# A graph kernel whose own planner orders its instructions: other durations in the planner's table

## Chip, cores and metric

The kernel runs on one core of one Trainium2 chip. The metric is device time in microseconds for one execution; the time given for the kernel before is the median of three runs. Besides those, one execution was profiled.

The core has five engines that each run their own instruction stream in order and wait for each other by semaphores: TensorE (PE in the profile, its weight loads PEld), VectorE (DVE), ScalarE (ACT), GpSimd (POOL) and SyncE (SP). Here GpSimd does little but issue indirect DMAs, and SyncE little but issue ordinary ones.

## What is computed

There are 16 graphs of 1024 nodes with 64 features each, and an adjacency matrix of 1024 x 1024 float32 per graph, about eight neighbours to a node. Four layers follow each other, each on a layer-normed and rectified copy of the features, each added to the features:

```python
h = jnp.maximum(_layernorm(x, axis=-1), 0.0)
x = x + _L0_gnn_ref(h, adj, W)             # (adj @ h) @ W.T
h = jnp.maximum(_layernorm(x, axis=-1), 0.0)
x = x + _L1_gnn_ref(h, adj, ...)           # m = mlp(h); msg = relu(adj @ m); a gated unit of (msg, h)
h = jnp.maximum(_layernorm(x, axis=-1), 0.0)
x = x + _L2_gnn_ref(h, adj, weight, K, b)  # Chebyshev: h, adj @ h, 2 adj @ (adj @ h) - h
h = jnp.maximum(_layernorm(x, axis=-1), 0.0)
x = x + _L3_gnn_ref(h, adj, nodemask, ...)
```

The last layer thins each node's list of neighbours (in lists of more than ten every k-th is removed, in both directions), takes for each feature the quartiles over the values of the neighbours left, with weights 1/4, 1/2 and 1/4, adds them to the node's own value and runs a small two-layer network.

## The kernel before

**Stages of a graph.** Each stage is a Python generator (a "chain") that yields one instruction at a time.

- *Transposing* (`transposing`): eight blocks of the adjacency matrix are loaded by SyncE into two buffers (`block`), transposed by TensorE and copied by ScalarE into tiles `AT`, of which there are 15; a graph takes eight.
- *Coding* and *listing* (`coding`, `lists`): the sign of the transposed tiles is packed into words, and VectorE finds from them the up to 24 neighbours of each node (`top`, `cand`, `more`, then three MAX8 and two MATCH_REPLACE8 for each of eight row tiles, then some forty small instructions, the last of which writes `many`). This is called the list block below. A graph's list is made some graphs ahead of its use. After the last one, `longest` finds the nodes with long lists.
- *Layers* (`layers`): two chains, one for the even and one for the odd graphs, run layers 0 to 2. A chain holds one tile `X` and ends with the last sum `pay<-X,bank` on VectorE, a norm on ScalarE, and the stores of `table` and `rows` by SyncE. The next graph of the chain begins with the load of `X`. Three passes over a graph's eight `AT` tiles (`bank<-AT,nodes`) are in it; the third gives the tiles back.
- *Gathering* (`gathering`, `gathers`): GpSimd gathers for each graph ten neighbours of eight row tiles from `table`, 80 indirect DMAs, into one of two buffers `G`, slot after slot.
- *Quantiling* (`quantiles`): VectorE begins with `hits<-G,pay`, runs a sorting network of min and max over slots of 128 x 512 values, ping-pong between `G` and the one buffer `net`, and ends with the coefficients `coef<-off`. Then the sorted slots are weighed by the coefficients (six instructions on VectorE, 24 on ScalarE).
- *Dense* (`dense`): TensorE sums the weighed slots (`bank<-G,c`), after which `G` is given back, and runs the small network; the result is stored by SyncE (`out<-yo`), and one of three `pay` buffers is given back.
- *Long lists*: at the end the nodes with more than eleven neighbours, gathered from all graphs (`whom`), pass through gathering, quantiling and dense again in four batches with longer networks; that is 122 more gathers, and nine scatters of results.

**What sets the order.** The class `Weave` is a planner that runs while the kernel is built. It keeps a clock for every engine. Each chain offers its next instruction; the earliest start of an instruction is the later of the time at which its engine is free (`free`) and the time at which its operands are ready (`ready`). The engine on which something can start earliest is served; among the instructions that could start on it within `SLACK` (0.1 us) of that, the one whose chain has the lowest key wins. Keys are graph numbers with an offset: layers and transposing `b - 3`, coding the same, listing `b - 2`, dense `b`, gathering and quantiling `b + 1`; so a layer of graph 7 goes before a quantile instruction of graph 4.

An instruction has two numbers: `cost`, for which it occupies its engine, and `later`, the time after that until its result can be used. Use on another engine adds 0.15 us. `Line.cost` gives both for each kind of instruction; a gather has its own, `GATHER`: it occupies GpSimd for so long, and lands 2.2 us later. Each instruction is made in the planned order and tied to the one before it on its engine:

```python
for other in self.last.get(line, ()):
    self.behind(ins, other)
```

So the order on every engine is the planner's, while the times at which instructions really run come from the hardware. In the kernel before, VectorE and ScalarE instructions have a `cost` and no `later`.

In the profile nearly every instruction bears line 303, the line at which a chain's instruction is made; tiles tell them apart. Gathers have line 634, stores line 640 and scatters line 1324.

Of the kernel before, what the change touches and what calls it, by code (L numbers as in the profile page):

```python
# [98 lines left out]
EXTRA = 6 * NT  # L99
BIG = 1e30  # L100
SLACK = 0.1
GATHER = 1.33
RANK = 3.0
SHARE = 3
LONGEST = 512
# [74 lines left out]
def network(n, places, beam=200):  # L180
# [4 lines left out]
    for layer in needed(batcher(n), range(places)):  # L185
        new = {}
        for buf, (cost, ops) in states.items():
            classes = {}
            for a, b, la, lb in layer:
# [73 lines left out]
class Op:  # L263
# [5 lines left out]
    def __init__(self, line, make, writes, reads, cost, later=0.0, after=()):  # L269
        self.line, self.make, self.cost, self.later, self.after = line, make, cost, later, after  # L270
        self.writes, self.reads = [place(a) for a in writes], [place(a) for a in reads]
# [16 lines left out]
class Line:  # L288
# [17 lines left out]
    def cost(self, method, out, reads, kwargs):  # L306
        if method == "dma_start":
            return 0.4, 2.0 + out.nbytes() / 150e3
        n = max(a.free_size() for a in [out] + reads)
        extra = "accum_out" in kwargs  # L310
        if self.name == "DVE":
            fixed = {"match_replace": 0.145, "max": 0.155}.get(method, 0.155)
            return fixed + n / 960 + 0.08 * extra, 0.0
        if self.name == "ACT":
            scalars = sum(hasattr(kwargs.get(k), "ap") for k in ("bias", "scale"))
            return 0.225 + n / 1400 + 0.09 * scalars + 0.19 * extra, 0.0
        if self.name == "PE":
            if method == "transpose":
                return 0.19, 0.25
            n = out.free_size()  # L320
            if mybir.dt.size(reads[0].dtype) == 2:
                return 0.06 + n / (4400 if out.shape[0] == C else 2200), 0.3
            pair = n == 512 and reads[0].shape[0] == P and out.shape[0] == C
            return (0.58 if pair else max(0.34, 0.06 + n / 545)), 0.3
        return 1.33, 2.2


# [140 lines left out]
class Fast:  # L468
# [162 lines left out]
    def gather(self, out, table, at, reads):  # L631

        def make():
            return self.nc.gpsimd.indirect_dma_start(  # L634
                out=out, out_offset=None, in_=table, in_offset=bass.IndirectOffsetOnAxis(ap=at, axis=0))
        return Op(self.G, make, [out], [reads, at], GATHER, 2.2)

# [1345 lines left out]
```

## Time and profile before

| | us |
|---|---|
| median of three runs (lowest, highest) | 2125.57 (2113.96, 2135.73) |
| the profiled execution | 2138.34 |
| its span, from first to last instruction | 2136.4 |
| first gather starts | 130.9 |
| last gather starts | 2092.2 |

| engine | busy us |
|---|---|
| PE | 1533.9 |
| PEld | 717.0 |
| DVE | 1632.9 |
| ACT | 1073.5 |
| POOL | 1437.7 |

The mean granted clock of TensorE was 0.782 of full speed. Durations are of one profiled execution. A line of a timeline gives the start, the duration, the engine, the source line, the operation, what it writes and reads, and in brackets the idle time of the engine before it with the event that ended it. A merged line (x4) has the duration from the first start to the last end. An instruction's own duration overlaps that of its neighbour on VectorE and ScalarE, so a sum of durations is more than the time the engine needs for them.

### The profile page before, as it was taken

The numbers are of one execution on the slowest core, as the hardware profiler recorded it, in microseconds if no ns is written. First come the engines' busy times: TensorE is split into PE (matmuls) and PEld (weight loads), VectorE is DVE, ScalarE is ACT, GpSimd is POOL, SyncE is SP. The second block draws the span as 40 slices with busy tenths as digits, with TensorE's granted clock in tenths as the row PEclk, the third lists the DMA queues.
The fourth block names the chain that finished last, engine by engine and source line by source line (L and its number), as shares of the span: only waits on it lengthen the run. The fifth ranks groups of instructions, "written<-read, shape, count | busy, mean of one in ns | idle before, by whom it ended". The sixth has DMA issues, their size and how long they took to land. (4 is left out here: it accounts for less than half of the span.)

```text
span 2136.4 us, 22993 instructions
## 1 busy us (share of the span) xinstructions
PE 1533.9 (72%) x6172; PEld 717.0 (34%) x6172; DVE 1632.9 (76%) x4293; ACT 1073.5 (50%) x2921; POOL 1437.7 (67%) x1441
## 2 busy tenths in 40 slices
PE   6978677869787879787887878787978872233303
PEld 2443323333434343343333333334343331111302
DVE  2661687978888887888886969787788899949646
ACT  3654647566666655566656474757466532011000
POOL 2047776777676767577777667676757777776772
PEclk9979796978788796989796979787779786555555
DMA  4242625252625252444334353525252314121110
GB/s 121 70 86 57 117 38 94 59 105 52 104 51 104 52 93 58 58 94 61 88 62 94 50 94 61 104 48 99 51 92 50 43 31 41 30 31 24 32 27 11
DMA packets 246840, 140.93 MB, mean 66 GB/s; under 512 B 76048, under 2 KB 223952, under 8 KB 246704
## 3 DMA queue, kind: packets, MB, share of 16 engines
q1 hardware_dynamic: 195664, 88.11, 18.4%
q0 software_dynamic: 46096, 48.62, 17.5%
q10 hardware_dynamic: 4944, 2.66, 0.5%
q8 instruction: 53, 0.87, 0.2%
q14 instruction: 83, 0.68, 0.1%
HBM read 120.10 MB, written 19.17 MB: 65 GB/s over the span
## 5 line engine op out<-in xcount | busy, mean ns | idle before, releaser
L634 POOL DMA_INDIRECT G<-table,pay x1402 | 1408.0, 1004 | 652.6 <-issue 351.6
L303 PE MATMUL bank<-AT,nodes 128*64 128x512 f32 x2048 | 605.7, 671 | 88.1 <-ACT nodes L303 78.6
L303 PEld LDWEIGHTS bank<-AT,nodes 128*64 128x64 f32 x2048 | 181.6, 153 | 386.2 <-issue 223.6
L303 PE MATMUL bank<-G,c 128*128 128x512 f32 (+3 forms) x382 | 172.1, 590 | 183.4 <-DVE G L303 179.4
L303 PE MATMUL bank<-c,block 128*128 128x128 f32 x976 | 223.5, 349 | 106.8 <-DMA block<-in_adj 60.5
L303 ACT ACTIVATE AT<-bank 128x512 f32<-128x512 f32 x256 | 149.5, 588 | 188.9 <-PE bank L303 186.4
L303 PEld LDWEIGHTS bank<-c,block 128*128 128x128 f32 x976 | 147.3, 176 | 229.2 <-issue 137.7
L303 DVE TENSOR_TENSOR G<-G 128x512 f32<-128x512 f32 (+3 forms) x313 | 200.1, 674 | 2.8
L303 ACT ACTIVATE nodes<-X,off,ri 128x64 f32<-128x64 f32 x360 | 141.0, 429 | 42.6 <-DVE off L303 41.3
L303 DVE TENSOR_TENSOR net<-G 128x512 f32<-128x512 f32 (+6 forms) x240 | 150.6, 672 | 11.3 <-ACT G L303 9.3
L303 PEld LDWEIGHTS bank<-G,c 128*128 128x128 f32 x382 | 72.1, 226 | 254.5 <-DVE G L303 129.1
L303 ACT ACTIVATE G<-G,coef 128x64 f32<-128x64 f32 x384 | 98.2, 336 | 110.0 <-DVE coef L303 109.8
L303 ACT ACTIVATE sq<-X,st 128x64 f32<-128x64 f32 x360 | 124.6, 346 | 49.7 <-DVE st L303 34.1
L303 ACT ACTIVATE there<-AT 128x1024 f16<-128x1024 f32 x128 | 132.1, 1050 | 0.9
L303 ACT ACTIVATE wide<-bank 64x512 f32<-64x512 f32 x128 | 75.1, 586 | 108.7 <-PE bank L303 107.5
L303 DVE TENSOR_TENSOR G<-net 128x512 f32<-128x512 f32 (+7 forms) x189 | 117.2, 667 | 0.7
L303 DVE TENSOR_TENSOR G<-G,net 128x512 f32<-128x512 f32 (+3 forms) x177 | 111.4, 679 | 0.9
L303 PE MATMUL bank<-wide,wg 64*64 64x512 f32 (+1 forms) x192 | 110.1, 656 | 0.8 <-ACT wide L303 0.4
L303 DVE SCALAR_TENSOR_TENSOR G<-bad,G 128x512 f32<-128x512 f32 (+1 forms) x176 | 109.8, 693 | 0.0
L303 DVE MAX8 L<-cand 128x8 f16<-128x103 f16 x384 | 91.9, 263 | 8.8
L303 PE MATMUL bank<-there,c 128*64 128x512 f16 x256 | 79.8, 449 | 24.3 <-DVE there L303 24.1
L303 DVE TENSOR_REDUCE st<-X 128x8 f32<-128x512 f32 x48 | 32.9, 686 | 82.5 <-DMA X<-in_x 81.4
(200 smaller groups left out, 2235.0 us busy)
## 6 DMA issues: line engine op xcount, KB each, us to landing
block<-in_adj SPq DMA_DIRECT2D x121, 512.0 KB, 4.2
G<-table,pay POOLq DMA_INDIRECT x1402, 2.8
rows<-pay SPq DMA_DIRECT2D x16, 632.0 KB
table<-pay SPq DMA_DIRECT2D x16, 264.0 KB, 5.2
X<-in_x SPq DMA_DIRECT2D x16, 256.0 KB, 8.5
out<-yo SPq DMA_DIRECT2D x16, 256.0 KB, 2.6
G<-in_adj SPq DMA_DIRECT2D x3, 512.0 KB, 10.7
G<-in_adj ACTq DMA_DIRECT2D x3, 512.0 KB, 9.2
```

What stands on the lines that cost most here:

```text
L303: return Op(self, lambda: f(*args, **kwargs), writes, reads, cost, later)
L634: return self.nc.gpsimd.indirect_dma_start(out=out, out_offset=None, in_=table, in_offset=bass.IndirectOffsetOnAxis(ap=at, axis=0))
```

## The change

The planner's durations are set anew. No chain, key, buffer or instruction is written differently. For VectorE, ScalarE and the transposes, matmuls and gathers the time of occupation becomes shorter, and for VectorE and ScalarE a `later` of 0.09 and 0.10 us is split off.

```diff
-GATHER = 1.33
+GATHER = 1.29
...
         if self.name == "DVE":
-            fixed = {"match_replace": 0.145, "max": 0.155}.get(method, 0.155)
-            return fixed + n / 960 + 0.08 * extra, 0.0
+            fixed = {"match_replace": 0.165, "max": 0.095}.get(method, 0.07)
+            return fixed + n / 960 + 0.08 * extra, 0.09
         if self.name == "ACT":
             scalars = sum(hasattr(kwargs.get(k), "ap") for k in ("bias", "scale"))
-            return 0.225 + n / 1400 + 0.09 * scalars + 0.19 * extra, 0.0
+            return 0.13 + n / 1400 + 0.09 * scalars + 0.19 * extra, 0.1
         if self.name == "PE":
             if method == "transpose":
-                return 0.19, 0.25
+                return 0.165, 0.25
             n = out.free_size()
             if mybir.dt.size(reads[0].dtype) == 2:
                 return 0.06 + n / (4400 if out.shape[0] == C else 2200), 0.3
             pair = n == 512 and reads[0].shape[0] == P and out.shape[0] == C
-            return (0.58 if pair else max(0.34, 0.06 + n / 545)), 0.3
+            return (0.51 if pair else max(0.26, 0.06 + n / 640)), 0.3
         return 1.33, 2.2
```

For a VectorE instruction on 512 values a row, the planner's occupation goes from 0.688 to 0.603 us; the time until its result can be used stays nearly the same, 0.693.

## Prediction

> **What bounds the kernel now.** I read the page's busy shares first, then the waits, then GpSimd's, SyncE's and VectorE's timelines around two graphs.
>
> ```profile
> PE 1533.9 (72%) x6172; PEld 717.0 (34%) x6172; DVE 1632.9 (76%) x4293; ACT 1073.5 (50%) x2921; POOL 1437.7 (67%) x1441
> ...
> POOL 2047776777676767577777667676757777776772
> ...
> L634 POOL DMA_INDIRECT G<-table,pay x1402 | 1408.0, 1004 | 652.6 <-issue 351.6
> ```
>
> No engine is full, but GpSimd is never long idle after the first tenth. A gather is 1.00 us busy and, at "issue", 0.25 us more (351.6/1402), so 80 of a graph need at least 100 us. In the timeline the gathers of graphs 4, 9 and 14 (counted from 0) begin at 566.65, 1121.21 and 1683.98: 111 to 113 us a graph. The one at 1683.98, in the order of time from SyncE, GpSimd and VectorE (start, duration, engine):
>
> ```profile
> 1676.98 0.37 SPq L640 DMA_DIRECT2D table<-pay  x1
> ...
> 1683.98 0.94 POOL L634 DMA_INDIRECT G<-table,pay  x1 [3.03 <-DVE more L303]
> ...
> 1792.53 1.15 POOL L634 DMA_INDIRECT G<-table,pay  x1 [1.49 <-DVE net L303]
> ```
>
> GpSimd waits for graph 14's table, whose store was issued 7.0 us earlier (the VectorE name in brackets is only the last event). From there GpSimd runs to its last gather at 2092.2 with few waits, the longest 9.28 us, and the kernel ends 44 us later. So the layers of a graph (in pairs, through all engines) set the pace until 1684, and GpSimd sets the end from there. VectorE at graph 9, then at 14:
>
> ```profile
> 1106.26 0.68 DVE L303 TENSOR_TENSOR pay<-X,bank 128x512 f32<-128x512 f32 x1
> ...
> 1107.77 0.45 DVE L303 TENSOR_REDUCE coef<-off 128x72 f32<-128x288 f32 x1
> ...
> 1116.18 0.68 DVE L303 SCALAR_TENSOR_TENSOR cand<-top,c 128x504 f16<-128x504 int32 x1 [3.26 <-ACT cand L303]
> ...
> 1125.93 0.69 DVE L303 TENSOR_REDUCE st<-X 128x8 f32<-128x512 f32 x1 [6.10 <-DMA X<-in_x]
> ...
> 1149.59 0.17 DVE L303 TENSOR_TENSOR many<-dil,notes 128x8 f32<-128x8 f32 x1
> ...
> 1159.91 0.33 DVE L303 TENSOR_TENSOR hits<-G,pay 128x160 f32<-128x160 f32 x1 [0.21 <-DMA G<-table,pay]
> ...
> 1667.51 0.68 DVE L303 TENSOR_TENSOR pay<-X,bank 128x512 f32<-128x512 f32 x1
> ...
> 1670.83 0.45 DVE L303 TENSOR_REDUCE coef<-off 128x72 f32<-128x288 f32 x1
> ```
>
> The last sum of graph b (`pay<-X`) and the end of graph b-2's quantiles (`coef`, after which G is only weighed and read) fall together. Then comes the list block of a later graph, alone, up to `many`, with VectorE waiting inside it; then `hits`, the next quantiles. Hence G of graph b-2 comes free just when the table of graph b lands.
>
> **The change, part by part.** No instruction is added or removed on VectorE (4,039 in both programs), TensorE or GpSimd; ScalarE gets 35 instead of 33 table loads. The rest is order, so I compared the order of the two built programs engine by engine, and priced what is moved by its rows here.
>
> *Pay earlier.* Ahead of the last sum of graph 9 stand 23 network instructions fewer, 14.0 us by their own records (a 128x512 one starts 0.60 us after its neighbour; the page's mean of 0.69 overlaps it); for graphs 5 to 14 it is 13 to 17 us. It is one shift, not one per graph: with the pace unchanged it gives the table nothing that GpSimd can use, because of the next item.
>
> *Quantiles later.* Ahead of `coef` of graph 7 stand 107 instructions more, nearly all one list block: 24 MAX8 5.7 us, 16 MATCH_REPLACE8 4.0 and their value loads 1.5 (16 x 92 ns), 8 short MAX8 1.1, five wide ones 2.9, 41 small 8.1, 13 of layers and coding 3.6: 26.9 us. Other graphs have 106 to 110 more, graphs 5 and 9 only 39. `coef` of graph 12 has 142 more: 23 of layers 9.2, the list block 23.5 (same rows), and 25 of the step that finds the long rows, 12.4: 45.1 us. `hits` has next to none more before graph 12, so the same quantile work is spread over the list block.
>
> *Who waits for that.* Gathers of graph b write G of graph b-2, slot by slot. Graph 15 shows how far ahead they may run: they began at 1792.5, `coef` of graph 13 at 1800.5, 8.0 us. For graph 9: coef 7 at 1107.8 + 26.9 - 8.0 = 1126.7 against 1121.2 now; a delay of some 5 us, covered, since `hits` of that graph comes later still. For graph 14 nothing covers it: 1670.8 + 45.1 - 8.0 = 1707.9 against 1684.0, **24 us later**. If VectorE keeps waiting at its present rate in the moved block (94 us busy of 110 a graph: 33.4 + 60.1 in two windows), 45.1 becomes 52.8 and the delay 32. I take 24, the value nearest to records of the very instructions. After that all is GpSimd: graph 15 follows 14 without a hold (`coef` of 13 has only 2.0 us more ahead), and the tail's order on VectorE is the same from `coef` of 13 on. So +24 us passes to the end.
>
> *Pace.* What the layers' chain gains or loses is unpriced by any row. Above nothing: the list block's waits, X 81.4 us and `cand` 37.2 us over 16 graphs, 7.4 a graph, may be filled by network work that now stands there. Below: between the last sum and the next graph's first layer sum, VectorE's own work was 7 to 10 us and becomes 12.5 to 16.8 in most graphs (+5 to +7), while the rest of the loop shrinks from 80.5-82.7 to 74-79 (-3 to -8). The two nearly cancel, so I take zero; ends -6 to +3 us a graph over the 12 graphs from 2 to 14.
>
> *Queues.* SyncE: in five graphs a block load now stands between the rows' store and the next X load; it waits for TensorE to leave its buffer (1149.7 us in 119 waits, 9.7 each), and X behind it, and VectorE at `st<-X`: 0 to 49 us, taken at 0 since X is used late; it is part of the slower rival. GpSimd: one gather and one scatter change places in the tail, within 1 us. Two more table loads are 2 x 1.28 us on an engine half idle: 0, 2.6 without that cover. PE's order changes in thousands of places; its share is in the pace.
>
> [...] Gathers took 0.95 us each beside the list block (30.53/32, 660 to 705 us) and 0.99 beside the network (51.39/52, 705 to 772). If all 30 of the former met network work, a graph would lose 1.0 us, 12 in all; as the number of network instructions is the same, I take 0. [...]
>
> *Sum.* The profiled execution took 2138.3 us (span 2136.4), 12.8 above the median of the runs. 2138.3 + 24 = 2162 on its scale, 2125.6 + 24 = **2150** for the median; own range 2138 to 2165.
>
> **Rivals.** *Faster: the list block's waits are filled.* For it: VectorE stands 7.4 us a graph in that block, and network work is placed around it. Against: part of it is waiting for the layers' own chain, which no order shortens. GpSimd's floor is some 104 us a graph (graph 10's gathers ran 1237.2 to 1340.2 plus issue) against 110, so at most 6 x 12 = 72. With 4.5 a graph: 2125.6 + 24 - 54 = 2096; at most 2078. It decides above 2 us a graph (24/12).
>
> *No change: pace pays for the delay.* 1 to 3 us a graph saved: -12 to -36, 2126 in the middle. Against: it needs a coincidence.
>
> *Much slower: the layers' chain itself gets longer,* by 3 us a graph from the 5 to 7 us more between the two sums, with X late in five graphs: 24 + 36 = 60, 2186. Against: the shorter rest.
>
> That the order would not change is excluded: VectorE's two lists differ in most places.
>
> **Numbers.** Within 1% (2104 to 2147) is about what a measurement here can't tell from no change. Forecast 0.38, faster 0.29, no change 0.20, much slower 0.13. The forecast's range begins inside the 1% band: 0.05 of its 0.38 goes there. Faster 0.29, same 0.25, slower 0.46. The range drops a tenth on each side: the fastest third of the gain (below 2088) and the end of the much slower case (above 2186).
>
> **What would show it.** `coef` of graph 7 after a list block and some 27 us later against `many`; GpSimd's start of graph 14 held by G, not by the table store, some 24 us after 1684; tables 110 us apart; the tail from there as long as now (452 us from 1684 to the end). It would be wrong if tables came 107 us apart or less, or 113 or more; if waits for X and `cand` on VectorE vanished and the pace followed; or if gathers could run much further than 8 us ahead of `coef`.

## The result, and the profile after

The changed kernel takes 2235.3 us (median of four runs, 2215.77 to 2238.58) beside 2126.7 for the kernel before in the same session (2113.96 to 2135.73): a ratio of 1.0496, with a 95% interval of 1.0415 to 1.0577. Between the two medians lie 108.6 us, more than four times the 24 that were forecast, and the time is outside of the range.

| profiled execution, us | before | after | difference |
|---|---|---|---|
| span | 2136.4 | 2232.0 | +95.6 |
| tables of graph 4 to 14, per graph | 111.7 | 117.4 | +5.8 |
| store of graph 14's table | 1677.0 | 1732.5 | +55.5 |
| from that store to the graph's first gather | 7.0 | 53.2 | +46.2 |
| first gather of graph 14 | 1684.0 | 1785.8 | +101.8 |
| from there to the end (the tail) | 452.4 | 446.2 | -6.2 |

So up to graph 14 a hundred microseconds were lost, about half of them in the distance of the tables and half in a wait of GpSimd behind the last of them, and the tail gave 6 back. Below, this wait is called the hold: the time from the store of a graph's table to its first gather. It is not at graph 14 alone: from graph 3 to 13 it is 28 to 41 us in the changed kernel and 5 to 9 in the kernel before.

Distances, holds and tails are read from one profiled execution of each kernel. Those of the kernels on ordinary chips lie from 12 us below to 15 above the median of their kernel's runs, and the kernel before was profiled 12 us above its own. By these numbers I estimate some 1 us a graph of uncertainty in each distance, and small differences between distances are not read.

The page of the changed kernel, its busy times, GpSimd's row of the 40 slices and the gathers' group:

```profile
PE 1558.6 (70%) x6172; PEld 715.5 (32%) x6172; DVE 1628.1 (73%) x4293; ACT 1077.2 (48%) x2923; POOL 1426.4 (64%) x1441
...
POOL 2047677737676757767676757675757477776772
...
L634 POOL DMA_INDIRECT G<-table,pay x1402 | 1396.3, 996 | 757.6 <-issue 337.9
```

VectorE and GpSimd work no longer than before: 1628.1 us against 1632.9, and 1426.4 against 1437.7. ScalarE has 3.7 us more, and TensorE 24.7 (1558.6 against 1533.9) with the same number of instructions. The span is 95.6 us longer. What GpSimd has more is idle time before its gathers, 757.6 against 652.6, and the idle time put down to "issue" is less (337.9 against 351.6).

The list of waits of the changed kernel (us in total, times, longest):

```profile
POOL G L634 <- PE bank L303: 118.6, 45, 16.3
PE bank L303 <- DMA block<-in_adj: 116.6, 28, 9.2
...
POOL G L634 <- DVE net L303: 95.2, 7, 30.5
...
DVE of_h L303 <- ACT wide L303: 73.8, 13, 12.3
```

Before, GpSimd waited 13.9 us for `bank`, 10.8 for `net` and 37.9 for its tables; for tables it now waits 0.3. It waits for the instructions that read or write `G` last: dense's matmuls and the sorting network. That is the hold by the buffer that the prediction named. The second line belongs to transposing and the fourth to the layers; they stood at 60.5 us (10 times) and 23.8 before.

Graph 14 in the timelines of SyncE, GpSimd and VectorE of the changed kernel:

```profile
1722.86 0.69 DVE L303 TENSOR_TENSOR pay<-X,bank 128x512 f32<-128x512 f32 x1 [1.41 <-PE bank L303]
...
1732.53 0.37 SPq L640 DMA_DIRECT2D table<-pay  x1
...
1785.78 1.15 POOL L634 DMA_INDIRECT G<-table,pay  x1 [23.94 <-DVE net L303]
...
1792.28 0.44 DVE L303 TENSOR_REDUCE coef<-off 128x72 f32<-128x288 f32 x1
```

The last sum of graph 14 and the end of graph 12's quantiles, which stood 3.3 us apart before, are 69.4 apart. The table has long landed (by the page, 4.7 us after its issue in the median) when GpSimd's first gather starts, 53.2 us after that store and 6.5 us before `coef`.

Where the other half went is read from the windows view, each kernel from its table 4 to its table 14. After the window and its length come the busy times with the numbers of instructions, then the granted clock, the DMA share and GB/s; the kernel before first.

```profile
560.20:1677.00 1116.80, 925.95 (x3664) 422.43 (x3663) 916.54 (x2440) 678.99 (x1869) 795.52 (x797) 0.82 0.41 74
```

```profile
558.10:1732.50 1174.40, 937.53 (x3656) 422.90 (x3656) 905.83 (x2436) 681.67 (x1869) 797.21 (x801) 0.79 0.43 71
```

VectorE (the third busy time) does nearly the same work in both, 916.5 and 905.8 us for ten graphs. It is idle for 200.3 us of the first and 268.6 of the second. The 57.6 us that ten graphs take longer are idle time of VectorE, 68.3 more, less 10.7 of busy time. The same view from the start to the first gather of graph 14, before and after:

```profile
0.00:1683.98 1683.98, 1371.94 (x5522) 627.80 (x5522) 1286.33 (x3528) 996.47 (x2686) 1128.64 (x1141) 0.83 0.41 76
```

```profile
0.00:1785.78 1785.78, 1413.50 (x5600) 632.87 (x5600) 1310.79 (x3649) 1016.88 (x2736) 1123.01 (x1142) 0.80 0.42 72
```

Of the 101.8 us up to that gather VectorE is busy for 24.5 and idle for 77.3.

### The profile page after: what moved, and what is told of

Its sections match the earlier page's. It is cut to its first block, busy times and chain, and to the rows that moved or that the text cites. A ratio compares the mean times of both kernels' runs of the same rounds, so it can differ in the third digit from the quotient of the medians.

```text
span 2232.0 us, 23001 instructions
## 1 busy us (share of the span) xinstructions
PE 1558.6 (70%) x6172; PEld 715.5 (32%) x6172; DVE 1628.1 (73%) x4293; ACT 1077.2 (48%) x2923; POOL 1426.4 (64%) x1441
## 5 line engine op out<-in xcount | busy, mean ns | idle before, releaser
L634 POOL DMA_INDIRECT G<-table,pay x1402 | 1396.3, 996 | 757.6 <-issue 337.9
L303 PE MATMUL bank<-G,c 128*128 128x512 f32 (+3 forms) x382 | 183.9, 604 | 209.9 <-DVE G L303 209.9
L303 PE MATMUL bank<-c,block 128*128 128x128 f32 x976 | 225.8, 360 | 142.2 <-DMA block<-in_adj 116.6
L303 PEld LDWEIGHTS bank<-AT,nodes 128*64 128x64 f32 x2048 | 167.3, 153 | 379.6 <-issue 235.0
L303 ACT ACTIVATE G<-G,coef 128x64 f32<-128x64 f32 x384 | 95.6, 336 | 102.3 <-DVE coef L303 102.0
L303 DVE SCALAR_TENSOR_TENSOR of_h<-bank,bhn,wide 64x512 f32<-64x512 f32 x32 | 23.8, 744 | 121.3 <-ACT wide L303 73.8
L303 PE MATMUL bank<-wide,wg 64*64 64x512 f32 (+1 forms) x192 | 101.1, 616 | 2.9 <-ACT wide L303 2.0
L303 DVE TENSOR_TENSOR net<-G,net 128x512 f32<-128x512 f32 (+3 forms) x140 | 87.4, 665 | 0.1
```

What stands on the lines that cost most here:

```text
L303: return Op(self, lambda: f(*args, **kwargs), writes, reads, cost, later)
L634: return self.nc.gpsimd.indirect_dma_start(out=out, out_offset=None, in_=table, in_offset=bass.IndirectOffsetOnAxis(ap=at, axis=0))
```

## Experiments

The prediction had the quantiles late in the order and took the pace of the layers (the distance of the tables) as unchanged. The theory after the result: the late quantiles themselves cost the pace, some 6 us a graph, besides the hold of GpSimd at graph 14. Against it stood that the shorter durations spoil the order in some other way, by VectorE's and ScalarE's numbers (the title of the change) or by TensorE's; that a shift of the quantiles is harmless where the layers are undisturbed; and that the time goes inside one tie or one engine.

To choose kernels I read the order that each would have, with VectorE's work summed between two points (us of work; no time is in it). Two numbers describe it: how far `coef` of graph b-2 stands behind the last sum of graph b, and how far the last sum of graph b stands behind `yo` of graph b-3, which frees its `pay` buffer.

```
                                      coef behind last sum   pay free ahead
before                                      -1 to 3             31 to 33
after                                       23 to 52             5 to 15
after, TensorE's numbers old                -5 to -3            31 to 63
before, TensorE's numbers new               37 to 53             4 to 5
before, one TensorE number new              36 to 49             5 to 13
after, that number 0.58, 0.60, 0.62         -5 to 11            32 to 36
after, AT = 13 in place of 15                7                   31
```

There are two kinds of order, and one number decides between them: the 0.58 us of a pass's matmul, which became 0.51. The layers have the lower key. My reading is that with cheaper passes they run ahead in the plan and VectorE's quantile work is put off, until the three `pay` buffers stop the layers; the last sum then stands 5 us behind the freeing of its buffer. The table fits this, but it does not show the planner's single decisions.

**TensorE's numbers old, the rest new.**

```diff
-                return 0.165, 0.25
+                return 0.19, 0.25
...
-            return (0.51 if pair else max(0.26, 0.06 + n / 640)), 0.3
+            return (0.58 if pair else max(0.34, 0.06 + n / 545)), 0.3
```

> The kernel before with the new durations for VectorE, ScalarE and the gather, and the old ones for TensorE. On VectorE the coefficients of graph b-2 then stand within 5 us of graph b's last sum, as before, and the pay buffer of graph b-3 is free 31 to 63 us of VectorE work ahead of its next use. Theory A (only the matmul and transpose durations tip the plan into late quantiles, and these cost the time): within 1.5% of before, tables some 110 us apart. Rival B (the split of VectorE's and ScalarE's time, which gives the change its name, costs it): 3 to 5% slower, tables 115 to 118 us apart.

2142.1 us, ratio 1.011 (1.0027 to 1.0193); tables 112.6 us apart, the first gather of graph 14 4.8 us after its table, tail 448.0. In this order the new split of VectorE's and ScalarE's durations, which names the change, and the gathers' new number cost about a fifth of the loss (0.3 to 1.9%). The last two runs have the same new numbers and no loss, so it is not a price that they always have.

**The opposite: the kernel before with TensorE's numbers new.** The same lines the other way round.

> The kernel before with the new durations for TensorE alone. The coefficients of graph b-2 stand 37 to 53 us of VectorE work behind graph b's last sum (23 to 52 in the changed kernel), the pay buffer comes free 5 us ahead of its use. Theory A: 4 to 6% slower, tables 116 to 119 us apart, GpSimd's start of a graph held by G. Rival B: within 1.5% of before.

2225.2 us, ratio 1.0509 (1.0435 to 1.0584); tables 116.9 us apart, hold at graph 14 57.0, tail 452.5. All of the loss is there.

**The changed kernel with the key of the quantiles and of dense lowered by two, ahead of the layers.**

```diff
-            c = dict(T=NT, n=NEAR, PS=self.paid[b], key=float(b) + 1.0, graph=b)
+            c = dict(T=NT, n=NEAR, PS=self.paid[b], key=float(b) - 1.0, graph=b)
```

> The changed kernel with the key of quantiling and dense lowered by two, so that they go before the list block. All new durations stay. The coefficients of graph b-2 stand 25 us of VectorE work ahead of graph b's last sum, the pay buffer is free 88 us ahead. Theory A: the loss is gone, within 2% of before, GpSimd held by the table and not by G. Rival C (the order inside the layers, made from the shorter matmul times, costs the time, not the place of the quantiles): still 3 to 5% slower. Rival D (quantile work put ahead of layers delays these): slower too, but with the layers' steps longer where network instructions stand in them.

2299.5 us, ratio 1.0878 (1.0803 to 1.0953): slower still. Theory A, which expected the loss to be gone, missed here, and rival D held. The hold is gone (4.4 us at graph 14) and GpSimd waits for its tables; the waits of this kernel:

```profile
POOL G L634 <- DMA table<-pay: 229.6, 12, 23.5
```

The tables are 122.3 us apart. With the quantiles first, layer steps on VectorE stand behind them: from the end of the second layer (the second `X<-X,hn` of a graph) to the first operand of the third layer's second pass (`nodes<-nodes,kc,bank`) the layers' chain takes 37.7 us a graph on average over graphs 4 to 13, and 19.3 before. Quantiles too early cost more here than quantiles too late; what the kernel before has is a middle.

**The kernel before, all durations old, with the quantiles' key raised,** which makes the late order without touching a duration. The edit raises the key of quantiling and of dense by 1.5; that of gathering, which the expectation names too, stays.

```diff
-            c = dict(T=NT, n=NEAR, PS=self.paid[b], key=float(b) + 1.0, graph=b)
+            c = dict(T=NT, n=NEAR, PS=self.paid[b], key=float(b) + 2.5, graph=b)
```

> The kernel before, all old durations, with the key of gathering and quantiling raised by 1.5, so that lists and layers go before them further ahead. The coefficients of graph b-2 stand 20 to 33 us of VectorE work behind graph b's last sum, the pay buffer comes free 5 us ahead of its use: the same state of the plan as in the changed kernel, without any of its durations. Theory A: 3 to 5% slower, tables 115 to 118 us apart, GpSimd's start of graph 14 held by G for 30 to 50 us after the table. Rival C: within 1.5% of before.

2193.1 us, ratio 1.0364 (1.0293 to 1.0434); tables 116.1 us apart, hold at graph 14 20.8 (30 to 50 expected), tail 450.2. Its windows view from table 4 to table 14, and its first gather of graph 14 in GpSimd's timeline, with the table stored at 1732.46:

```profile
571.90:1732.50 1160.60, 929.61 (x3726) 440.34 (x3725) 926.21 (x2479) 718.11 (x1900) 799.64 (x802) 0.81 0.40 70
```

```profile
1753.21 1.15 POOL L634 DMA_INDIRECT G<-table,pay  x1 [19.68 <-DVE net L303]
```

VectorE is idle for 234.4 us, 34.1 more than before. Old durations and a late order: most of the pace is lost as in the changed kernel (4.4 of 5.8 us a graph), so the late order needs none of the new durations to cost it.

**One number alone.** The kernel before with 0.51 for 0.58, and the changed kernel with 0.62 for 0.51.

```diff
-            return (0.58 if pair else max(0.34, 0.06 + n / 545)), 0.3
+            return (0.51 if pair else max(0.34, 0.06 + n / 545)), 0.3
```

> The kernel before with one number changed: the planner's time for a matmul of the passes over the adjacency goes from 0.58 to 0.51 us. On VectorE the coefficients of graph b-2 then stand 36 us of work behind graph b's last sum and the pay buffer comes free 5 us ahead of its use, from graph 5 on. Theory A (a plan with late quantiles and no slack on the pay buffers costs the time, whatever brings it about): 3.5 to 5.5% slower, tables 115 to 118 us apart. Rival E (the sum of many wrong prices costs it, each a little): less than 2% slower.

2243.9 us, ratio 1.0527 (1.0475 to 1.0579); tables 119.8 us apart (115 to 118 expected), hold 30.5, tail 473.0. This one number makes the whole loss, though with a smaller hold and a longer tail than in the changed kernel.

```diff
-            return (0.51 if pair else max(0.26, 0.06 + n / 640)), 0.3
+            return (0.62 if pair else max(0.26, 0.06 + n / 640)), 0.3
```

> The changed kernel with one number changed: the planner's time for a matmul of the passes goes from 0.51 to 0.62 us, all other new durations stay. The plan is then as in the kernel before: coefficients within 5 us of the last sum, pay buffer free 34 to 44 us ahead. Theory A: within 1.5% of the kernel before, tables 110 to 113 us apart. Rival E: 3 to 5% slower, as the changed kernel.

2129.4 us, ratio 1.0007 (0.998 to 1.0033); tables 110.5 us apart, hold 5.1. And this one takes it away.

**The step that finds the long rows put later.** It stood in what was to make `coef` of graph 12 late (12.4 of 45.1 us).

```diff
-RANK = 3.0
+RANK = 1.0
```

> The changed kernel with the step that finds the long rows at a later key (15 in place of 13). On VectorE the coefficients of graph 12 stand 42 us behind graph 14's last sum in place of 52; all else up to there is the same. If that step is what holds GpSimd longer at graph 14 than at the graphs before it (53 us after the table store against 28 to 38), the hold there falls to 40 to 45 us and the time to 0.3 to 0.6% under the changed kernel's, 4.3 to 4.7% over the kernel before; the tables stay 117 us apart. If the pace alone decides, no change against the changed kernel (5.0%).

2224.0 us, ratio 1.0442 (1.0401 to 1.0484). The hold at graph 14 is 31.7 us in place of 53.2, the tail 456.7 in place of 446.2, and the tables stay at 117.5. That step is worth some 21 us of the hold (8 to 13 expected), half of which comes back in the tail, and the pace does not change with it. The ratio is as expected, but its interval overlaps that of the changed kernel (1.0415 to 1.0577), so the total does not show the gain.

**The list block's key raised,** so that the quantiles would go ahead of it.

```diff
-LIST_KEY = -2
+LIST_KEY = 0
```

> The changed kernel with the list block's key raised by two, so that quantiles go before it but still after the layers. Coefficients stand 14 to 30 us of VectorE work ahead of the last sum, the pay buffer is free 61 to 84 us ahead. Theory A: the loss is gone, within 2% of before. If lists now come too late for the layers (Rival D, as in the run with quantiles before the layers): slower than 3%, GpSimd waits for tables, not for G.

26224.7 us. The page shows 226,025 instructions, most of them from lines 1547 to 1909: the kernel's general path, which runs after the fast one when its flag is raised. Why it was raised I did not find out, and the run says nothing on the order.

**Four kernels on another chip.** The changed kernel with fewer `AT` tiles, and the changed kernel with room made for a fourth `pay` buffer, without and with it:

```diff
-AT = 15
+AT = 13
```

> All durations as changed, only AT = 13 in place of 15, so that transposing runs two tiles less far ahead. In the order built from it VectorE's work puts coef of graph b-2 7 us behind the last sum of graph b (23 to 52 in the changed kernel, -1 to 3 before) and the last sum 31 us behind the freeing of its pay buffer (5 in the changed kernel, 32 before). Theory A, the order's late quantiles are the cause and the durations only the way into it: tables 110 to 113 us apart from graph 4 to 14, gathers start 4 to 9 us after their table, total 2105 to 2150, ratio 0.99 to 1.015. Rival, the shorter TensorE durations spoil the order in another way (transposes or block loads at a bad place): still 116 us or more a graph, ratio 1.035 to 1.055. Rival, two tiles fewer cost the passes their lead: 113 to 116 us a graph with holds of 4 to 9, ratio 1.015 to 1.035.

```diff
-AT = 15
+AT = 14
```

> As the changed kernel with AT = 14. The order built from it has coef of graph b-2 5 to 10 us behind the last sum up to graph 7 and 21 to 53 from graph 8 on, and the pay buffer freed 32 us ahead up to graph 7, 15 to 17 for 9 and 10, 3 to 6 from 11 on. Theory A with the tie: within one run the tables are 110 to 113 us apart from 4 to 8 and 115 to 120 from 11 to 14, holds 5 to 10 first and over 25 later; total between: ratio 1.015 to 1.04. Rival, pace goes with the durations, not with the order: one pace over the whole run, 116 to 118.

```diff
-        stock("wide", 3, [P, N])
+        stock("wide", 2, [P, N])
...
-        stock("yo", 2, [P, NT * C])
+        stock("yo", 1, [P, NT * C])
```

> The changed kernel with two wide tiles in place of three and one yo in place of two, to make room; VectorE's order is as in the changed kernel. It is the base of the next run. Ratio 1.04 to 1.06, tables 116.5 to 118.5 us apart, last sum 4 to 6 us after the result of graph b-3 is stored.

```diff
-PAYS = 3
+PAYS = 4
```

> The run before with PAYS = 4: a last sum waits for the pay buffer of graph b-4, not b-3, and nothing else is loosened. The quantiles stay late in the order: coef of graph b-2 12 to 55 us behind the last sum. Theory, the pace is lost because the layers are tied through the pay buffer to the late results: tables 110 to 113.5 us apart, holds 25 to 70 us, ratio 1.01 to 1.03. Rival, the pace is lost inside the layers (dense's matmuls and network work between their steps, block loads late): tables 116 us or more apart, ratio 1.04 to 1.06, though the last sum now starts up to 10 us before the store of graph b-3's result or far from it.

Here the kernel before itself took 3267.0 us, and the four 3324.4, 3334.6, 3345.4 and 3316.5: ratios of 1.018, 1.022, 1.025 and 1.015. The distances expected in us don't apply where every graph takes 182 to 186. The intervals of the four overlap, so they decide nothing between the theory and its rivals; another wait rules there (the last section). The same four again, on a chip like the first ones:

> All durations as changed, AT = 13, as in the run of this kernel on the chip where the kernel before took 3267 us; here the question needs a chip on which the kernel before takes some 2125 us. Theory A, the order's late quantiles cost the time: tables 110 to 113 us apart from graph 4 to 14, holds 4 to 9 us, ratio 0.99 to 1.015. Rival, the shorter TensorE durations spoil the order elsewhere: 116 us or more a graph, ratio 1.035 to 1.055. Rival, two AT tiles fewer cost the passes their lead: 113 to 116 us with holds of 4 to 9, ratio 1.015 to 1.035.

2154.8 us, ratio 1.0194 (1.015 to 1.0238). Tables 111.9 us apart and graph 14 held for 4.5 us, both as expected of the order in time; but the total lies above 1.015, where the second rival had it. The tail is 467.5 us long, 15 more than before, with graph 15 held for 27.1 (17.3 before). Two tiles fewer undo the loss of pace and cost something at the end, which I did not follow up. All durations are the changed ones here.

> The base of the next run, the changed kernel with two wide tiles and one yo: tables 116.5 to 118.5 us apart, last sum 4 to 6 us after the store of graph b-3's result, ratio 1.04 to 1.06.

2222.7 us, ratio 1.0527 (1.046 to 1.0594); tables 115.8 apart (116.5 expected), last sums 4 to 5 us after the store of graph b-3's result in most graphs.

> The run before with PAYS = 4. Theory, the pace is lost in the tie of the layers to late results through the pay buffer: tables 110 to 113.5 us apart, holds 25 to 70 us, ratio 1.01 to 1.03. Rival, it is lost inside the layers (dense's matmuls and network work between their steps, block loads late): tables 116 us or more apart, ratio 1.04 to 1.06, with the last sums no longer tied to the store of graph b-3's result.

2202.3 us, ratio 1.0417 (1.0372 to 1.0462). The last sums now start from 11 us before that store to 25 after it, so the tie is loosened. Over all ten graphs the tables are 114.4 apart, between the two expectations; but from graph 4 to 12 they are 115.7 apart, and 115.8 without the fourth buffer. Only graphs 13 and 14 come faster, 109.2 against 116.0. The windows view of the two, without and with the fourth buffer:

```profile
552.90:1711.30 1158.40, 944.66 (x3656) 427.56 (x3656) 905.05 (x2436) 681.02 (x1869) 794.92 (x799) 0.79 0.42 72
```

```profile
556.50:1700.00 1143.50, 950.95 (x3680) 419.75 (x3680) 907.84 (x2431) 680.52 (x1872) 791.55 (x800) 0.81 0.42 73
```

VectorE is idle for 253.4 and 235.7 us. The fourth buffer gives back 20 us of the 109 lost on this chip, so the tie through three buffers is a small part. Up to graph 12 the pace is as slow with the fourth buffer as without. That this part is lost inside the layers, as the rival has it, is what remains when the tie is excluded; it is not shown.

> The changed kernel with AT = 14: quantiles in time up to graph 7, late from 8 or 9 on, the last sums close behind the freeing of their pay buffer from 11 on. Theory A: tables 110 to 113 us apart from 4 to 8, 115 to 120 from 11 to 14, ratio 1.015 to 1.04. Rival, the pace goes with the durations and not with the order: one pace of 116 to 118 over the whole run.

2174.9 us, ratio 1.0302 (1.0255 to 1.0349). Within this one run, the tables of graphs 4 to 8 are 108.7 apart with holds of 5 to 7 us, and those of 10 to 14 are 114.0 apart with holds of 28 to 39. From 11 to 14 they are 112.4 apart, less than the 115 to 120 that I expected, and from 8, where the order turns late, to 10 they are 110.2 apart. Taken over all of the late part, 8 to 14, it is 112.7 against 108.7: the distance grows where the order changes, with one set of durations, but the late part is only 1 us a graph above the kernel before. This run supports the theory weakly.

**The changed kernel with that one number left as it was, 0.58, and with 0.60.**

```diff
-            return (0.51 if pair else max(0.26, 0.06 + n / 640)), 0.3
+            return (0.58 if pair else max(0.26, 0.06 + n / 640)), 0.3
```

> The changed kernel with one number left as it was before, 0.58 for a matmul of a pass in place of 0.51. In the order built from it coef of graph b-2 stands -1 to 3 us from the last sum of graph b up to graph 11 and 8 to 11 after that, the pay buffer free 32 to 36 us ahead. Theory A (the late order costs the time, and this number is the way into it): tables 108 to 112 us apart, holds 5 to 10 us, ratio 0.985 to 1.01. Rival, the other shorter numbers cost something by themselves, as in the run with TensorE's old ones (1.011): ratio 1.01 to 1.03.

2108.9 us against 2113.6, ratio 0.998 (0.9947 to 1.0012). Its windows view from table 4 to table 14, and its first gather of graph 14 in GpSimd's timeline (table stored at 1634.03):

```profile
553.70:1634.00 1080.30, 898.60 (x3657) 400.75 (x3656) 908.71 (x2430) 670.23 (x1868) 792.67 (x800) 0.85 0.40 77
```

```profile
1639.37 0.94 POOL L634 DMA_INDIRECT G<-table,pay  x1 [4.78 <-DVE whole L303]
```

VectorE's work is nearly the same again, 908.7 us, and its idle time 171.6; the tables are 108.0 us apart. The hold is 5.3 us. The profiled execution is the fastest of twelve, 12 us under the median, so these distances flatter the kernel a little; over all runs it is as fast as the kernel before.

> The same with 0.60. Order in time throughout, coef -5 to 3 us from the last sum, pay buffer free 33 to 36 us ahead. Theory A: as at 0.62 and 0.58, tables 108 to 112 us apart, ratio 0.985 to 1.01; a version that beats both kernels would stand under 0.99. Rival, small differences of order move the pace by several us whatever the regime: ratio outside of 0.985 to 1.015, or the runs at 0.58, 0.60 and 0.62 more than 1.5% apart.

2102.3 us, ratio 0.9953 (0.9931 to 0.9974); tables 108.5 us apart, hold 7.4, tail 446.7. Of all versions this is the only one whose interval lies below that of no change, by half a per cent; that is less than the 1% that the expectation asked of a better version, and it was the best of three values tried. At 0.58, 0.60 and 0.62 the ratios are 0.998, 0.995 and 1.001, within 0.6% of each other, as the theory had it.

## Why the prediction was wrong

**The mechanism of the hold was the right one.** `coef` of graph 7 came after a list block, GpSimd's start of graph 14 was held by `G` and not by the table's store, gathers ran 6.5 us ahead of `coef` (8.0 taken), and the tail stayed as long as it was within 6 us. The direction followed from that, but only half of the loss did: the other half came from the pace, which the sum had at zero. The prediction also had the delay of the graphs before 14 covered (some 5 us at graph 9); the hold at graph 9 was 32.0 us, where it had been 6.0.

**The marker on `coef` of graph 7 was badly put.** It is 57 us later against `many`, not 27: it stood 41.8 us ahead of it and now stands 15.6 behind. The 26.9 us are the block's own instructions; in the trace the block also holds waits and other chains' work. The delay was reckoned from work and not from `many`, so the time does not rest on it.

**The step that failed is "Pace": "The two nearly cancel, so I take zero".** The tables came 117.4 us apart, beyond both ends (-6 to +3 us a graph; measured +5.8) and beyond the 113 that the prediction itself named as a sign of being wrong. The working shows how the error sits in waiting. `coef` of graph 12 moved from 1670.83 to 1792.28, by 121.4 us. The prediction counted 45.1 us of instructions ahead of it. From the start to that `coef` VectorE is busy for 39.6 us more (1316.96 against 1277.33) and idle for 81.8 more. Before, the first gather of graph 14 came 13.2 us after `coef`, now 6.5 ahead: 121.4 - 13.2 - 6.5 = 101.7, what was measured. The forecast was 45.1 - 13.2 - 8.0 = 24. The work was forecast within 6 us; the difference is waiting, and the view that shows it is that of VectorE's busy and idle time.

I reached the zero by adding up VectorE's work on the loop of the layers before and after. Work on one engine did not set that loop here: over ten graphs VectorE's work fell by 10.7 us, and the loop took 57.6 more. The loop passes through three engines that each run their streams in the planned order, so a step waits for what stands ahead of it there. An order that puts another phase of the quantiles beside the layers can change those waits without changing any sum of work; the list of waits shows that they did change, and not how they add up.

**The hold was sized nearly right.** It grew by 46.2 us. The 24 us of the forecast were reckoned against a table that stays at its time, although the last sum stands 13 to 17 us of work earlier in the order; against an earlier table the same reckoning gives 37 to 41. Some 5 to 9 us were missing there.

**Pay earlier.** The prediction said that it gives GpSimd nothing. That held, as the table came 55 us later and not 14 earlier.

**The much slower rival** had the right outcome, a longer loop of the layers, at half its size (3 us a graph), and 0.13 of the chance. Its reasons were others: it had more work between the two sums and `X` late, but VectorE's work over a whole loop did not grow, and its waits for `X` fell. The reason given against it, "the shorter rest", did not hold.

**The faster rival** took waits for `X` and `cand` to be filled by network work. The waits for `cand` did vanish (37.2 to 2.7 us), and `st<-X` fell from 81.4 to 49.7 us. But others took their place: `of_h` waiting for ScalarE (23.8 to 73.8 us) and TensorE (16.8 to 54.4), and TensorE waiting for block loads (60.5 to 116.6).

**Contention of gathers and network** was priced at up to +12 us and taken at zero. The gathers' mean went from 1004 to 996 ns, so no such loss shows.

**Why the planner made the late order** was not asked in the prediction, which took the order from the built program. The runs answer it: the one TensorE number is the way in. The new number is not plainly a better or a worse measurement. A graph has four passes over its `AT` tiles (the third layer has two, so the last pass is the fourth and not the third), which makes 1024 planned matmuls in the kernel, and the trace has 2048 records of them, two for each. In the kernel before, records that follow each other without idle time start 0.261 us apart on average, 0.52 us for two, which is nearer to 0.51. The group's busy time, 605.7 us, is 0.59 us for each planned matmul, which is nearer to 0.58. With 0.51 the plan is late, with 0.58 it is in time, and on the chip the late one cost 6 us a graph.

**What stays open** is which waits make up the 6 us. No single one goes with the pace through all the runs: block loads cost TensorE 116.6 us in the changed kernel and 60.5 before, but 60.8 in the kernel with old durations and late quantiles, which has lost the pace too; `of_h` behind ScalarE costs 73.8 in the changed kernel and 50.6 in the kernel at 0.58, which has not. With four `pay` buffers the stretch from the first operand of the third layer's second pass to the last sum takes 16.3 us a graph in place of 19.4 (17.3 before; averages of graphs 4 to 13), and the pace to graph 12 is the same. That the order with late quantiles costs the pace is shown by the runs in which one key or one number makes it or takes it away; how the cost divides among the waits is not shown.

## What to carry to other kernels

A planner's durations are inputs to an order, not measurements to be set right one by one: a single number moved by 0.07 us tipped the plan into another kind of order here. So after each one see where the producers and consumers of a buffer stand to each other, and keep a number that holds a good order. When instructions move and none is added, don't price the move by the work on one engine: count, over a stretch of several graphs, the busy and the idle time of the engine that all chains share. Here the work was forecast well and the error sat in the idle part. Where a shared engine's work is due in the middle between two loops, putting it earlier and putting it later can both cost time (8.8% and 3.6% here).

## What the runs showed of the hardware

On one chip all five kernels that ran there took half as long again, the one before 3267 us in place of some 2120, while VectorE's instructions kept their durations. The group of the short MAX8 of the list block, first in the changed kernel on an ordinary chip, then in the one with 13 `AT` tiles there (busy, mean ns, idle before):

```profile
L303 DVE MAX8 L<-cand 128x8 f16<-128x103 f16 x384 | 91.9, 263 | 8.6
```

```profile
L303 DVE MAX8 L<-cand 128x8 f16<-128x103 f16 x384 | 91.7, 263 | 522.5 <-remote 394.8 <-issue 115.4 <-DVE cand L303 9.9
```

Each MAX8 takes its 263 ns, but VectorE waits 522.5 us before them. The profile puts 394.8 us of that down to "remote" and names no instruction. The timeline from 1098 to 1128 us has waits of up to 3.2 us on VectorE, 18.1 on ScalarE and 18.8 on TensorE, while GpSimd's gathers start their usual 1.25 us after each other. What holds the engines there is open.

The same trace shows the granted clock beside TensorE's use. Two stretches of 50 us of that run, the first between gathers, the second beside them (first busy time PE, then PEld, DVE, ACT, POOL; then the clock):

```profile
1000.00:1050.00 50.00, 39.72 (x175) 16.52 (x176) 47.95 (x93) 23.85 (x68) 0.00 (x0) 0.90 0.13 37
...
1100.00:1150.00 50.00, 10.25 (x26) 4.19 (x26) 11.88 (x59) 10.01 (x27) 25.55 (x28) 0.50 0.19 40
```

At 39.7 us busy the clock is 0.90, at 10.3 it is 0.50; the three other stretches from 1000 to 1250 us have 15.2, 40.4 and 41.0 us at 0.64, 0.84 and 0.91. The rows show the two beside each other, not what sets the clock. In the study's own windows from table 4 to 14 the clock was 0.85 in the kernel at 0.58, 0.82 before and 0.79 after, with TensorE busy for 898.6, 926.0 and 937.5 us with nearly the same number of instructions, 0.246, 0.253 and 0.256 us for each. The largest group of matmuls, the passes', has a mean of 669, 671 and 677 ns in the three traces. So a part of the lost pace may be slower matmuls. I estimate at most 1.2 us a graph of the 5.8 here, as TensorE's busy time grew by 11.6 us in ten graphs; no run separates this part.
